# Selective-scan Mamba on one core: a later norm product, softplus's 1 + u in PSUM, the gate behind the scans, and another order of TensorE's work

## The chip, the cores and the metric

The kernel runs on 1 core of a Trainium2 chip. The metric is device time in microseconds (us), the median of the runs of one kernel. All arithmetic is fp32. The engines are TensorE (PE; its weight loads are PEld), VectorE (DVE), ScalarE (ACT), GpSimd (POOL) and SyncE (SP), whose queue issues nearly all DMAs.

## The reference

Four layers run one after the other on x of shape (4, 96, 64, 64): a fusion of two Mamba blocks (L0), a four-direction SSD Mamba (L1), the first kind again (L2), and a ConvNeXt block (L3). The change touches L0 and L2 alone. Each of these applies two Mamba blocks (`sub` 0 and 1) to 4 sequences of L = 4096 tokens and C = 96 channels, with DIN = 192 inner channels, 16 states and dt rank 6:

```python
mu = seq.mean(-1, keepdims=True)
var = ((seq - mu) ** 2).mean(-1, keepdims=True)
h = (seq - mu) * jax.lax.rsqrt(var + EPS) * ln_g + ln_b
xs, z = jnp.split(h @ in_w, 2, axis=-1)
xc = jax.nn.silu(causal_conv4(xs) + conv_b)            # depthwise, 4 taps
dbl = xc @ xproj_w                                     # dt (6), Bm (16), Cm (16)
delta = jax.nn.softplus(dbl[..., :6] @ dt_w + dt_b)
dA  = jnp.exp(delta[..., None] * A)                    # (L, 192, 16)
dBx = delta[..., None] * Bm[:, :, None, :] * xc[..., None]
hstates = scan over tokens of  h = dA * h + dBx
y = jnp.einsum('blds,bls->bld', hstates, Cm) + Dp * xc
seq = seq + (y * jax.nn.silu(z)) @ out_w
```

After the two blocks come a 1 x 1 fusion with a pooled branch, a batch norm and the residual.

## The kernel before

**Steps and groups.** `mamba_fusion` runs 32 steps (2 pairs of sequences x 2 blocks x 8 chunks of T = 512 tokens), so the two fusions have 64. A step treats two sequences at once: 2 x 192 channels are laid out as three tiles `j` of 128 rows. With 16 states, a step has 3 x 128 x 16 rows to scan. They are cut into 24 *groups* of 2 x 128 rows (`units`: tile j, then q = 0 to 3, then p = 0, 1), and the loop in `Scan.run` gives each group one *slot*. Groups with q even and p = 1 (`dma`, six of 24: numbers 1, 5, 9, 13, 17, 21) get their delta x input by a broadcasting DMA, the others by a TensorE matmul.

**What a group needs.** `load` (SP) fetches delta, broadcast over the states, into `da` (8 buffers), five slots ahead. `decay` (ACT, two slots ahead) makes exp(delta A). `spread` (one slot ahead) makes `bs` in PSUM (two tiles): four PE records at L343 or, for a dma group, two exps on ACT. `product` (POOL, L351) is for the dma groups. `scan` (DVE) multiplies `bs` by B (L369) except in dma groups, and runs two hardware scans (L374) into `hs` (4 buffers). One slot later `after` multiplies by C on POOL (L381, `hc`, 4 buffers). `sums` (PE, L400, three slots behind the scan) adds the states up into `py`, one PSUM bank, which serves one tile j at a time; for the last q it adds the D term (L394). When a tile is through, `close` (DVE, L408) reads `py` and gates it with silu(z), in place in `xz`. After j = 1 and j = 2, `project` (PE, L416 and L418) multiplies by `out_w` into the `po` bank, and `keep` (ACT, L425 or L569) brings that back to the sequence X in SBUF. `spread_out` and `reload` serve the second block only.

**The front.** In the same slots a generator, `mamba_front`, prepares the next step. The loop advances it `PACE[slot]` times a slot, where slot 0 lies LEAD slots ahead of the step's end. It centres by a matmul (`pc`), squares (ACT, L194), takes the variance by a matmul (`pv`, L184, in the `po` bank), and the root as exp(-0.5 ln) on ACT (`rs`, L111). DVE multiplies `pc` by `rs` (L178), and POOL applies gain and bias (L179). Then come 12 tap matmuls with the convolution folded into `in_w` (`pu`, L205, copied to `xz` by ACT at L210), three for z (`pz`, L215), x_proj (`pd`, L228; `dbl`), and three dt matmuls (`pt`, L269) with a softplus each. These matmuls use two `mm` banks in turn. [...]

**Softplus.** `softplus` (ACT) makes u = exp(-|x|), t = ln(1 + u), and w = 1 + u (L291). One slot later `softplus_rest` (DVE) makes max(x, 0) + t (L297) and what rounding lost in w (L299: `lg<-wa,ua`); POOL adds the two (L251), multiplies by the input (L252), and SP stores both to DRAM (`dd`, `dg`, L246), from where `load` reads them.

**What sets the order.** It is written out by hand: at the end of a slot every traced instruction is tied behind the one before it on its engine,

```python
if ins.engine in last:
    self.tc.add_manual_dep(ins, last[ins.engine].name, IN_ORDER, reason="order")
```

so each engine runs in the order in which `run` calls the stages. An engine that waits holds everything behind it.

Of the kernel before, what the change touches and what calls it, by code (L numbers as in the profile page):

```python
# [18 lines left out]
F32 = mybir.dt.float32  # L19
AF = mybir.ActivationFunctionType  # L20
ALU = mybir.AluOpType
# [4 lines left out]
B, C, HH, WW = 4, 96, 64, 64  # L26
L = HH * WW
P = 128
T = 512
# [97 lines left out]
def rsqrt(act, out, in_, eps):  # L127

    act.exp_ln(out, in_, AF.Ln, bias=eps)
    act.exp_ln(out, out, AF.Exp, scale=-0.5)  # L130
# [28 lines left out]
def mamba_front(tc, k, X, pools, wt, pair, c, h, made):  # L159

    nc = tc.nc
    work, psum, dram = pools
    if c == 0:
        nc.vector.memset(h[:C, :, 0:3], 0.0)
    else:
        nc.scalar.copy(h[:C, :, 0:3], h[:C, :, T : T + 3])

    def bank(name):
        return psum.tile([P, T], F32, tag="mm", name=name)

    centered, roots = [], []
    for n in range(4):
        if n >= 2:
            dst = h[:C, n - 2, 3 : 3 + T]
            nc.vector.tensor_tensor(dst, centered[n - 2][0], roots[n - 2], ALU.mult)  # L178
            nc.gpsimd.tensor_scalar(  # L179
                dst, dst, wt["ln"][:, 0:1], wt["ln"][:, 1:2], ALU.mult, ALU.add  # L180
            )
        if 1 <= n < 3:
            pv = psum.tile([P, T], F32, tag="po", name="pv", bufs=1)[:C]
            nc.tensor.matmul(pv, lhsT=k.mean, rhs=centered[n - 1][1], start=True, stop=True)  # L184
            rs = work.tile([P, T], F32, tag="lg", name="rs", bufs=2)[:C]
            rsqrt(k.act, rs, pv, k.eps[:C])
            roots.append(rs)
        if n < 2:
            pc = bank("pc")[:C]
            nc.tensor.matmul(  # L190
                pc, lhsT=k.center, rhs=X[:, n, ds(c * T, T)], start=True, stop=True
            )
            sq = work.tile([P, T], F32, tag="ua", name="sq", bufs=2)[:C]
            nc.scalar.activation(sq, pc, AF.Square)  # L194
            centered.append((pc, sq))
        yield


    xz = made["xz"] = work.tile([P, 6, T], F32, name="xz", bufs=2)
    for j in range(3):  # L200
        pu = bank("pu")
        for tap in range(4):
            kk = C + 1 if tap == 3 else C
            for r0, r1, d0, d1, b in SEGS[j]:
                nc.tensor.matmul(  # L205
                    pu[r0:r1], lhsT=wt["conv"][:kk, tap, d0:d1], rhs=h[:kk, b, ds(tap, T)],
                    start=(tap == 0), stop=(tap == 3),
                )
            yield
        nc.scalar.copy(xz[:, j], pu)  # L210
    k.act.other(xz[:, :3], xz[:, :3], AF.Silu)
    for j in range(3):
        pz = bank("pz")
        for r0, r1, d0, d1, b in SEGS[j]:
            nc.tensor.matmul(  # L215
                pz[r0:r1], lhsT=wt["in"][:, DIN + d0 : DIN + d1], rhs=h[:C, b, 3 : 3 + T],
                start=True, stop=True,
            )
        yield
        nc.scalar.copy(xz[:, 3 + j], pz)  # L220


    dbl = work.tile([P, T], F32, name="dbl")
    pd = bank("pd")
    for n in range(2):
        for b in range(2):
            j, r0, r1 = ROWS[b][n if b == 0 else 1 - n]
            nc.tensor.matmul(  # L228
                pd[2 * QUART * b : 2 * QUART * (b + 1)], lhsT=wt["xproj"][r0:r1, j],
                rhs=xz[r0:r1, j], start=(n == 0), stop=(n == 1),  # L230
            )
    yield
    nc.scalar.activation(dbl, pd, AF.Identity, bias=wt["one"])
    yield


    rows = dram.tile([P, T], F32, name="rows")
    bc = made["bc"] = work.tile([P, 2, 2, T], F32, name="bc", bufs=2)


    du = made["du"] = work.tile([P, 3, T], F32, name="du", bufs=2)
    kept = []
    stores = [(rows, dbl)]
    for n in range(6):
        for stored in stores:
            nc.sync.dma_start(*stored)  # L246
        stores = []
        if 2 <= n < 5:
            j = n - 2
            delta, lost = kept.pop(0)[:2]  # L250
            nc.gpsimd.tensor_tensor(delta, delta, lost, ALU.add)  # L251
            nc.gpsimd.tensor_tensor(du[:, j], delta, xz[:, j], ALU.mult)  # L252
            for name, x in (("dd", delta), ("dg", du[:, j])):
                made[name, j] = dram.tile([P, T], F32, name=f"{name}{j}")
                stores.append((made[name, j], x))
        if 1 <= n < 4:
            softplus_rest(nc, *kept[-1])
        if n == 2:
            for b in range(2):
                for q in range(2):  # L260
                    r = HALFP * b + (QUART if q else RANK + 1)
                    nc.sync.dma_start(
                        bc[:, b, q], rows[r : r + NST, None].to_broadcast([NST, HEIGHT, T])
                    )
        if n < 3:
            pt = bank("pt")
            for r0, r1, d0, d1, b in SEGS[n]:
                half = ds(HALFP * b, HALFP)
                nc.tensor.matmul(  # L269
                    pt[r0:r1], lhsT=wt["dt"][half, d0:d1], rhs=dbl[half], start=True, stop=True,  # L270
                )
            kept.append(softplus(nc, k.act, work, pt))
        if n < 5:
            yield
    k.act.other(xz[:, 3:], xz[:, 3:], AF.Silu)

PACE = (1,) * 5 + (2, 1, 1, 1) * 2 + (2,) + (1,) * 10
LEAD = 5  # L280


def softplus(nc, act, work, x):

    u = work.tile([P, T], F32, tag="ua", name="ua", bufs=2)
    t = work.tile([P, T], F32, tag="lg", name="lg", bufs=2)
    nc.scalar.activation(u, x, AF.Abs)
    act.exp_ln(u, u, AF.Exp, scale=-1.0)
    act.exp_ln(t, u, AF.Ln, bias=1.0)
    w = work.tile([P, T], F32, name="wa", bufs=2)  # L290
    nc.scalar.activation(w, u, AF.Identity, bias=1.0)  # L291
    return work.tile([P, T], F32, name="delta", bufs=2), t, u, w, x

# [8 lines left out]
class Scan:  # L302
# [126 lines left out]
    def run(self, steps, wts, front, first):  # L429

        units = [(j, q, p) for j in range(3) for q in range(NQU) for p in range(2)]
        made = [first] + [{} for _ in steps[1:]]
        groups = [
            dict(
                pair=pair, sub=sub, c=c, wt=wts[sub], made=made[n], j=j, q=q, half=p, quarters=(p, p + 2),
                first=(q == 0 and p == 0), last=(q == NQU - 1 and p == 1),
                dma=(q % 2 == 0 and p == 1),
            )
            for n, (pair, sub, c) in enumerate(steps) for j, q, p in units
        ]  # L440
        total, each = len(groups), len(units)
        ahead = iter(())
        traced = self.tc.nc.cur_bb.bb.instructions
        last = {}
        for n in range(-5, total + 9):
            start = len(traced)
            slot = (n + LEAD) % each
            if slot == 0:
                for _ in ahead:
                    pass  # L450
                step = (n + LEAD) // each + 1
                ahead = front(step, made[step]) if 0 <= step < len(steps) else iter(())

            def at(lag):
                return groups[n - lag] if 0 <= n - lag < total else None

            if (g := at(4)) and g["last"]:
                self.close(g)
            for stage, lag in (
                (self.load, -5), (self.spread, -1), (self.decay, -2), (self.after, 1),  # L460
                (self.product, -2), (self.scan, 0), (self.sums, 3),
            ):
                if g := at(lag):
                    stage(g)

            for lag, what in (
                (4, self.project), (5, self.keep), (6, self.spread_out), (7, self.reload)
            ):
                if (g := at(lag)) and g["last"] and g["j"] and (g["sub"] or lag < 6):
                    what(g, g["j"] - 1)  # L470
            for _ in range(PACE[slot] if slot < len(PACE) else 0):
                next(ahead, None)

            for ins in traced[start:]:
                if ins.engine not in self.engines:
                    continue
                if ins.engine in last:
                    self.tc.add_manual_dep(ins, last[ins.engine].name, IN_ORDER, reason="order")
                last[ins.engine] = ins
# [1093 lines left out]
```

## Time and profile before

| | |
|---|---|
| Median of 3 runs | 10014.09 us (9990.49 to 10022.18) |
| Profiled execution | 9990.73 us, span 9989.0 us |
| Busy share: DVE, PE, POOL, ACT | 82%, 85%, 70%, 55% |
| DVE scans, L374, three largest forms | 2470.1 + 819.1 + 335.7 us |
| DVE products, L369 | 1397.3 us, 1152 of 1213 ns |
| POOL hc, L381 | 3664.1 us, 1536 of 2392 ns |
| PE spread, L343, and sums, L400 | 1518.7 us and 1737.8 us |
| DVE L299, L297 | 221.0 us (192 of 1151 ns), 129.9 us (192 of 677 ns) |
| DMA | 1531.94 MB, mean 153 GB/s |

A group's row gives its count, its total busy time and the mean of one, then the idle time of its engine just before it and what ended that. The shares are over the whole span; L0 and L2 must be read from windows. [...]

### The profile page before, as it was taken

Reading aid. Unit: us, or ns where it says so; the run is one execution under the profiler, and the core shown is the slowest. Engines: PE = TensorE matmul, PEld = TensorE weight load, DVE = VectorE, ACT = ScalarE, POOL = GpSimd, SP = SyncE. Lnnn points to the kernel's source line nnn. Section 1 sums busy time; section 2 is a strip of 40 time slices with the busy share of each in tenths; the row PEclk is TensorE's granted clock in tenths of the full one; section 3 lists DMA queues with packets and bytes.
Section 4 is the critical chain, followed back from the end, with each engine's and each line's share of the span. In section 5 each row is a group of like instructions: output and inputs, shape, how many; then the busy total and the mean of one; then the engine's idle time right before and its main releaser. Section 6 shows DMA issues by size and latency. Waiting matters only on the chain. (4 is left out here: it accounts for less than half of the span.)

```text
span 9989.0 us, 110219 instructions
## 1 busy us (share of the span) xinstructions
PE 8503.0 (85%) x32896; PEld 3493.9 (35%) x32896; DVE 8183.2 (82%) x10870; ACT 5509.4 (55%) x10786; POOL 6954.8 (70%) x4573
## 2 busy tenths in 40 slices
PE   7888888888886989898889898788888888888678
PEld 1112112111122776676766767111211112112122
DVE  7999999999996666766766667699899999899887
ACT  5565665655664455555555544456566565565345
POOL 6888888888885555555555556588888888888611
PEclk8989999999997998999999999799989999899889
DMA  7777777777775222322322221777777777777653
GB/s 188 190 197 195 205 206 198 198 193 195 205 195 151 69 70 79 86 66 82 88 66 77 82 71 49 181 195 200 194 203 204 200 199 190 197 200 198 171 118 84
DMA packets 813858, 1531.94 MB, mean 153 GB/s; under 512 B 126894, under 2 KB 132426, under 8 KB 809803
## 3 DMA queue, kind: packets, MB, share of 16 engines
q1 hardware_dynamic: 810186, 1519.79, 57.7%
q8 instruction: 260, 4.26, 0.2%
q10 hardware_dynamic: 3072, 5.11, 0.1%
q14 instruction: 340, 2.78, 0.1%
HBM read 1229.28 MB, written 148.50 MB: 138 GB/s over the span
## 5 line engine op out<-in xcount | busy, mean ns | idle before, releaser
L381 POOL TENSOR_TENSOR hc<-hs,bc 128x1024 f32<-128x1024 f32 x1536 | 3664.1, 2392 | 663.9 <-DVE hs L374 654.4
L374 DVE TENSOR_TENSOR_SCAN hs<-da,carry,bs 128x512 f32<-128x512 f32 x2016 | 2470.1, 1267 | 119.5 <-DVE bs L369 3.2
L343 PE MATMUL bs<-du,seldu 64*128 64x512 f32 x4608 | 1518.7, 713 | 719.4 <-DVE hs L374 719.2
L400 PE MATMUL py<-hc,selsum 128*32 128x512 f32 x6144 | 1737.8, 650 | 9.2 <-POOL hc L381 9.2
L111 ACT ACTIVATE da<-da,w_a 128x512 f32<-128x512 f32 x2304 | 1520.1, 710 | 0.7
L369 DVE TENSOR_TENSOR bs<-bs,bc 128x1024 f32<-128x1024 f32 x1152 | 1397.3, 1213 | 66.9 <-PE bs L343 66.9
L343 PEld LDWEIGHTS bs<-du,seldu 64*128 64x128 f32 x4608 | 406.6, 202 | 1702.7 <-DVE hs L374 1128.0
L351 POOL TENSOR_TENSOR du<-du,bc 128x1024 f32<-128x1024 f32 x384 | 933.0, 2430 | 0.0
L111 ACT ACTIVATE bs<-da,w_a 128x512 f32<-128x512 f32 x768 | 529.3, 689 | 712.1 <-DVE hs L374 699.6
L1020 DVE TENSOR_SCALAR seg<-dr,dac 128x128 f32<-128x128 f32 x1536 | 637.3, 448 | 285.3 <-PE y L1065 282.7
L1036 POOL TENSOR_TENSOR seg<-seg,cb 128x384 f32<-128x384 f32 x512 | 516.3, 1010 | 478.8 <-DVE cb L1035 408.6
L205 PE MATMUL pu<-h,w_conv 96*128 96x512 f32 (+3 forms) x2048 | 825.1, 628 | 1.4 <-POOL h L179 1.4
L374 DVE TENSOR_TENSOR_SCAN hs<-bs,carry,du 128x512 f32<-128x512 f32 x672 | 819.1, 1260 | 4.3
L971 PE MATMUL front<-pk,sconv 128*128 128x512 f32 x1536 | 754.0, 608 | 25.1 <-ACT z L959 20.6
L1075 POOL TENSOR_TENSOR y<-y,xs 128x192 f32<-128x192 f32 x496 | 295.9, 596 | 604.0 <-DVE y L1074 589.6
L1088 ACT ACTIVATE y<-yz 128x192 f32<-128x192 f32 x512 | 186.1, 364 | 904.1 <-DVE yz L1087 903.3
L400 PEld LDWEIGHTS py<-hc,selsum 128*32 128x32 f32 x6144 | 227.8, 111 | 1305.9 <-issue 677.3
L1040 POOL TENSOR_TENSOR xs<-pre,coef 128x576 f32<-128x576 f32 x512 | 598.6, 1174 | 53.5 <-ACT pre L116 24.8
L982 PE MATMUL front<-sconv,pk 128*128 128x192 f32 x3072 | 572.7, 330 | 56.1 <-DVE pre L987 50.6
L982 PEld LDWEIGHTS front<-sconv,pk 128*128 128x128 f32 x3072 | 497.1, 190 | 88.3 <-DVE pre L987 77.2
L1065 PEld LDWEIGHTS y<-xs,seg 128*128 128x128 f32 x3072 | 442.0, 206 | 142.2 <-issue 83.1
L1065 PE MATMUL y<-xs,seg 128*128 128x64 f32 x3072 | 446.7, 282 | 29.4 <-POOL seg L1036 23.9
(227 smaller groups left out, 13645.7 us busy)
## 6 DMA issues: line engine op xcount, KB each, us to landing
da<-dd SPq DMA_DIRECT2D x3072, 256.0 KB
du<-dg SPq DMA_DIRECT2D x768, 256.0 KB
dr<-rows SPq DMA_DIRECT2D x256, 384.0 KB
bc<-rows SPq DMA_DIRECT2D x256, 256.0 KB
dd<-delta SPq DMA_DIRECT2D x192, 256.0 KB
dg<-du SPq DMA_DIRECT2D x192, 256.0 KB
pk<-xn SPq DMA_DIRECT2D x128, 384.0 KB
pk<-xn SPq DMA_DIRECT2D x128, 256.0 KB
```

The lines of the kernel that those rows point to most:

```text
L111: self.last = self.scalar.activation(out, in_, func, **kw)
L205: nc.tensor.matmul(pu[r0:r1], lhsT=wt["conv"][:kk, tap, d0:d1], rhs=h[:kk, b, ds(tap, T)], start=(tap == 0), stop=(tap == 3),)
L343: nc.tensor.matmul(g["bs"][:, i], lhsT=self.sel["du"][rows, g["half"], g["q"]], rhs=g["made"]["du"][rows, g["j"]], start=True, stop=True,)
L351: self.tc.nc.gpsimd.tensor_tensor(g["du"], g["du"], self.b_or_c(g, 0), ALU.mult)
L369: nc.vector.tensor_tensor(dbx, dbx, self.b_or_c(g, 0), ALU.mult)
L374: nc.vector.tensor_tensor_scan(hs[:, i], da[:, i], dbx[:, i], init, ALU.mult, ALU.add)
L381: nc.gpsimd.tensor_tensor(g["hc"], hs, self.b_or_c(g, 1), ALU.mult)
L400: nc.tensor.matmul(py[rows], lhsT=self.sel["sum"][:, g["q"]], rhs=g["hc"][:, i], start=(g["q"] == 0), stop=(g["q"] == NQU - 1),)
L971: nc.tensor.matmul(p, lhsT=self.conv[:, i, DI + q * DST : DI + (q + 1) * DST], rhs=pk[:, i, ds(c * T, T)], start=(i == 0), stop=(i == 2),)
L982: nc.tensor.matmul(p, lhsT=pk[:, i, ds(c * Q, Q)], rhs=self.conv[:, i, :DI], start=(i == 0), stop=(i == 2),)
L1020: nc.vector.tensor_scalar(seg[:, h], g["pair"]["dr"][:, c % 2 * NH + h], made["dac"][:, n0 + h : n0 + h + 1], 0.0, ALU.subtract, ALU.min,)
L1065: nc.tensor.matmul(py[:, ch], lhsT=seg[:, h], rhs=xs[:, 0, ch], start=True, stop=True)
```

## The change

- In `mamba_front` the variance and roots come two turns behind the centring, and the product two turns behind the roots (six turns in place of four).
- `softplus` writes 1 + u into the PSUM bank `po` in place of an SBUF tile (`wa`).
- In the loop `close` moves behind `scan`. `keep`, `spread_out`, `reload` come one slot later and ahead of the front's work; `sums` moves behind the front's work, and `project` behind `sums` and one slot later.
- LEAD is 4 in place of 5, PACE follows, and the loop has one more slot at its end.

```diff
@@ -172,16 +172,16 @@
         return psum.tile([P, T], F32, tag="mm", name=name)
 
     centered, roots = [], []
-    for n in range(4):
-        if n >= 2:
-            dst = h[:C, n - 2, 3 : 3 + T]
-            nc.vector.tensor_tensor(dst, centered[n - 2][0], roots[n - 2], ALU.mult)
+    for n in range(6):
+        if n >= 4:
+            dst = h[:C, n - 4, 3 : 3 + T]
+            nc.vector.tensor_tensor(dst, centered[n - 4][0], roots[n - 4], ALU.mult)
             nc.gpsimd.tensor_scalar(
                 dst, dst, wt["ln"][:, 0:1], wt["ln"][:, 1:2], ALU.mult, ALU.add
             )
-        if 1 <= n < 3:
+        if 2 <= n < 4:
             pv = psum.tile([P, T], F32, tag="po", name="pv", bufs=1)[:C]
-            nc.tensor.matmul(pv, lhsT=k.mean, rhs=centered[n - 1][1], start=True, stop=True)
+            nc.tensor.matmul(pv, lhsT=k.mean, rhs=centered[n - 2][1], start=True, stop=True)
             rs = work.tile([P, T], F32, tag="lg", name="rs", bufs=2)[:C]
             rsqrt(k.act, rs, pv, k.eps[:C])
             roots.append(rs)
@@ -269,25 +269,25 @@
                 nc.tensor.matmul(
                     pt[r0:r1], lhsT=wt["dt"][half, d0:d1], rhs=dbl[half], start=True, stop=True,
                 )
-            kept.append(softplus(nc, k.act, work, pt))
+            kept.append(softplus(nc, k.act, work, psum, pt))
         if n < 5:
             yield
     k.act.other(xz[:, 3:], xz[:, 3:], AF.Silu)
 
 
 
-PACE = (1,) * 5 + (2, 1, 1, 1) * 2 + (2,) + (1,) * 10
-LEAD = 5
-
-
-def softplus(nc, act, work, x):
+PACE = (1,) * 6 + (2, 1) * 5 + (1,) * 8
+LEAD = 4
+
+
+def softplus(nc, act, work, psum, x):
 
     u = work.tile([P, T], F32, tag="ua", name="ua", bufs=2)
     t = work.tile([P, T], F32, tag="lg", name="lg", bufs=2)
     nc.scalar.activation(u, x, AF.Abs)
     act.exp_ln(u, u, AF.Exp, scale=-1.0)
     act.exp_ln(t, u, AF.Ln, bias=1.0)
-    w = work.tile([P, T], F32, name="wa", bufs=2)
+    w = psum.tile([P, T], F32, tag="po", name="w", bufs=1)
     nc.scalar.activation(w, u, AF.Identity, bias=1.0)
     return work.tile([P, T], F32, name="delta", bufs=2), t, u, w, x
 
@@ -442,7 +442,7 @@
         ahead = iter(())
         traced = self.tc.nc.cur_bb.bb.instructions
         last = {}
-        for n in range(-5, total + 9):
+        for n in range(-5, total + 10):
             start = len(traced)
             slot = (n + LEAD) % each
             if slot == 0:
@@ -454,22 +454,27 @@
             def at(lag):
                 return groups[n - lag] if 0 <= n - lag < total else None
 
-            if (g := at(4)) and g["last"]:
-                self.close(g)
             for stage, lag in (
                 (self.load, -5), (self.spread, -1), (self.decay, -2), (self.after, 1),
-                (self.product, -2), (self.scan, 0), (self.sums, 3),
+                (self.product, -2), (self.scan, 0),
             ):
                 if g := at(lag):
                     stage(g)
-
-            for lag, what in (
-                (4, self.project), (5, self.keep), (6, self.spread_out), (7, self.reload)
-            ):
-                if (g := at(lag)) and g["last"] and g["j"] and (g["sub"] or lag < 6):
-                    what(g, g["j"] - 1)
+            if (g := at(4)) and g["last"]:
+                self.close(g)
+
+            def completed(*stages):
+
+                for lag, what, subs in stages:
+                    if (g := at(lag)) and g["last"] and g["j"] and g["sub"] in subs:
+                        what(g, g["j"] - 1)
+
+            completed((6, self.keep, (0, 1)), (7, self.spread_out, (1,)), (8, self.reload, (1,)))
             for _ in range(PACE[slot] if slot < len(PACE) else 0):
                 next(ahead, None)
+            if g := at(3):
+                self.sums(g)
+            completed((5, self.project, (0, 1)))
 
             for ins in traced[start:]:
                 if ins.engine not in self.engines:
```

## The prediction

> **What bounds the kernel now.** I read the stage table first. The selective-scan part (the two `mamba_fusion` calls, about 100 to 3150 and 6400 to 9400 us) is two thirds of the span, and only it is touched. In it DVE is the busiest engine, and every engine is below its limit:
>
> ```profile
> 100.00:3000.00 2900.00, 2494.76 (x7600) 572.17 (x7598) 2647.72 (x2340) 1734.27 (x3249) 2437.49 (x1152) 0.91 0.75 198
> ```
>
> (Columns: length, busy us of PE, PEld, DVE, ACT, POOL, then clock, DMA share, GB/s.) DVE is busy for 91%, PE for 86%, POOL for 84%. Next, what DVE waits for, in the first fusion:
>
> ```profile
> DVE h L178 <- ACT rs L111: 70.1, 52, 3.1
> DVE xz L408 <- PE py L400: 53.1, 92, 4.5
> DVE bs L369 <- PE bs L343: 35.0, 53, 1.6
> DVE delta L297 <- ACT lg L111: 24.7, 30, 1.1
> ```
>
> The second fusion answers with 66.3, 60.1, 31.9 and 24.3. Together DVE stands 136 us at the norm's product, 113 at the gate, 67 at the scan's product and 49 at softplus: 365 us, 5.7 us for each of the 64 steps. A step takes 95.1 us (gate to gate, 3013.1 us for 760 groups of the first fusion, 24 groups a step). Third, the DVE timeline of one step, for what one group costs (start, duration, idle before):
>
> ```profile
> 1028.47 2.45 DVE L374 TENSOR_TENSOR_SCAN hs<-da,carry,bs 128x512 f32<-128x512 f32 x2
> 1030.84 2.43 DVE L374 TENSOR_TENSOR_SCAN hs<-bs,carry,du 128x512 f32<-128x512 f32 x2
> 1035.32 0.69 DVE L178 TENSOR_TENSOR h<-pc,rs 96x512 f32<-96x512 f32 x1 [2.04 <-ACT rs L111]
> 1036.84 1.23 DVE L369 TENSOR_TENSOR bs<-bs,bc 128x1024 f32<-128x1024 f32 x1 [0.83 <-PE bs L343]
> 1038.11 2.45 DVE L374 TENSOR_TENSOR_SCAN hs<-da,carry,bs 128x512 f32<-128x512 f32 x2
> ```
>
> From start to start a pair of scans takes 2.36 and a product 1.31, so a group costs 3.68, and 2.36 if it is one of the six of 24 fed by DMA. The 2.04 and 0.83 are one event. Fourth, PE's timeline tells why:
>
> ```profile
> 1014.64 2.08 PE L343 MATMUL bs<-du,seldu 64*128 64x512 f32 x4 [6.49 <-DVE hs L374]
> 1020.51 1.27 PE L343 MATMUL bs<-du,seldu 64*128 64x512 f32 x4
> 1032.74 1.10 PE L184 MATMUL pv<-sq,mean 96*96 96x512 f32 x2 [3.02 <-ACT X L569]
> ```
>
> The variance matmul `pv` shares the single `po` bank with `project`; it waits until ACT's `keep` has emptied it, ACT takes two roots' steps, and DVE, which owes the product one slot later, stands behind both. Behind its 6.49 us of idleness PE runs at half rate (2.08 for four records, then 1.27).
>
> [...] L299 (`w` and `u` in SBUF) takes 681 to 2890 ns, mean 1151; L297, the same form with one operand in PSUM, 662 to 693. Beside L299 POOL's `hc` takes 2.80 instead of 2.36. [...]
>
> **The change, part by part.** A group's slot is named by its number n in the step (0 to 23); the DMA groups are 1, 5, 9, 13, 17, 21.
>
> *Norm's product two slots behind its roots.* `pv` moves one slot further from `keep`, the roots stay with it, and L178 falls into slots 0 and 1, at least a whole slot after the second ACT step. ACT needs about 1.3 us for two steps, in a slot of 3.7. No instruction is added. Gain: all of the 136 us. POOL's L179 goes with it; POOL already waits there for DVE.
>
> *Gate at the slot's end.* L408 runs behind the scan of the same slot (2.4 to 3.7 us later), while its last sums were issued a slot before. In slots 3 and 19 PE is through; in 11 it is a tie. The cost is a wait of the next tile's first `sums` (one `py` bank) for this gate; `sums` and the next spread, about 2 us, fit into the following DVE slot. Gain 95 of 113; bounds 53 and 113.
>
> *1 + u in PSUM.* 192 instructions L299 of 1151 ns become like L297's 677: 192 x 0.474 = 91 us of DVE. [...] ACT's write to PSUM costs nothing: `bs<-da` takes 689 where `da<-da` takes 710. New wait: `w` of j+1 needs the bank that L299 of j reads, so ACT stands until that slot's end. Behind it on ACT are the exps of DMA group 17 (1.4 us), due a slot of 5 us later: covered. POOL's stretched `hc` come back to 2.36, off the path.
>
> *LEAD 4, new PACE.* The `dt` matmuls now follow slot 13, which has no front matmul, so ACT's logarithm is early: 40 of the 49 us at L297 go (bounds 0 and 49). Front, stores and loads of `bc` fall one slot later against the loads of `da`. On SP's queue the four `bc` loads (1 MB) now stand behind the two transfers of group 21 and right ahead of `dd`'s first store; that store frees the buffer that the third L297 writes, some 3 us later, where in the timeline shown there were 4.0 (1010.53 to 1014.54). That wait exists now (4.2 us, 4 times). I take 0.3 us a step, 19 us; bounds 0 and 1 us, 64.
>
> *Front's matmuls ahead of the sums, `project` a slot later.* The same work in another order; what comes late next is the spread. At full rate a spread is 1.06, a group's sums 0.98, a front matmul about 1.05, `project` 3.1: 77 us a step. From slot 2 to 12 PE holds 41 us against DVE's 39 (with one slot of lead), and slot 20, behind the gate of 19, 5.1 us. Added up slot by slot this leaves DVE 0.5 at group 6, 0.4 at 11, 1.1 at 22: 2.0 us a step[...]. Now it is 67/64 = 1.05. I take 2.2: 74 us more; bounds 0 and 205. ACT's copy of `pu` (L210) waits for `project` to free `xz`, 10.4 us a step now (312.1 in the first fusion) without hurting; that stays hidden.
>
> DVE work after it: 18 x 3.68 + 6 x 2.36 + 5 short ones (L178, L408) at 0.61 + 3 x (0.77 + 0.61) for softplus = 88 us; POOL 79, PE 77, so DVE stays the bound. DMA's 18.3 MB a step need 203 GB/s instead of 192; single windows of 4 us show 260 to 330, so loads stay covered. The extra slot at each fusion's end has only leftovers.
>
> **Sum:** 136 + 95 + 91 + 40 - 19 - 74 = 269 us. The profiled execution took 9990.7 (span 9989.0): 9722. The median of runs, 10014.1, lies 23 above it and the three spread over 32; I allow 8 and say 9730.
>
> **Rivals.** *A, PE becomes the bound.* For it: 77 of 90 us of work, dense stretches, half rate after waits; against it: PE waits 360 us for DVE in the first fusion alone. At the upper ends (205 and 64), with the gate at 53 and L297 at 0, it is 136 + 53 + 91 - 269 = 11 us: 9980 in this execution, 9988 in the median. Half of the way there, about 9860, is the likelier form.
>
> *B, ACT is caught behind `project`: slower.* L210 in slot 4 now stands in front of the exps of group 7, and `project` stands behind two front matmuls and the sums. PE's slots 2 to 4 hold 13.4 us from scan 1's end; exps of group 7 would be done at 15.3 and are due at 19.0. At half rate through all three slots PE ends at 26.8, exps at 28.7: 9.7 us lost a step, 621 in all, hence 9722 + 621 = 10343, 10350 as a median. It decides from a `project` 3.7 us late; from 8 us late the gain is gone. [...]
>
> *C, the waits only move.* If the DVE waits reflect an equal PE chain, they reappear at L369 and only L299's 91 us remain: 9900 in this execution, 9907 as a median.
>
> **How the numbers follow.** Forecast 0.58, A 0.20 (a fifth of it, 0.04, within 0.3% of no change), C 0.10, B 0.12 with any form that ends slower. A measurement of this kernel tells 0.3%, 30 us, from nothing. Faster 0.58 + 0.16 + 0.10 = 0.84, same 0.04, slower 0.12. The low end takes every saving whole, 136 + 113 + 91 + 49 = 389, and no new wait: 9602, say 9600. The high end, 9935, takes in C and most of A, and leaves out B and A's tail.
>
> **What would show it.** Right: L178's and L408's idle near nothing, L299 near 0.68 with a narrow spread, step of about 91 us, DVE above 94% in this stage. Wrong: idle at L369 above 250 us (A or C), L297 waiting for the store of `dd`, or exps on ACT with DVE's scan behind them and L210 waiting far over 10 us a step (B).

## The result and the profile after

The changed kernel is slower by 0.4%: 10046.9 us as a median (10025.03 to 10061.92, 14 runs) against 10009.18 of the kernel before (14 runs), a ratio of 1.0041, 95% interval 1.0031 to 1.0051. The forecast was 9730. The profiled execution's span is 10041.4 us, 52 above that of before; in the first fusion (100 to 3130 us) DVE is busy for 88%, where it was 91%.

What DVE waited for, first fusion, in the changed kernel (line waiting, what released it, us in total, times, longest), all but the smallest:

```profile
DVE bs L369 <- PE bs L343: 193.6, 70, 5.6
DVE delta L297 <- DMA dd<-delta: 81.5, 29, 4.1
DVE delta L297 <- POOL du L252: 4.3, 2, 2.2
```

The row of L299 among the groups (busy us, mean ns; 221.0 and 1151 before):

```profile
L299 DVE SCALAR_TENSOR_TENSOR lg<-w,ua 128x512 f32<-128x512 f32 x192 | 132.9, 692 | 20.4 <-ACT ua L111 0.5 <-DVE delta L297 0.5
```

The three waits that the change was aimed at are gone (L178's 136 us, 109 of the gate's 113, the 49 for ACT at L297), and L299 fell from 221.0 to 132.9 us. Two other waits took their place. In both fusions L369 waits 378 us for PE, where it was 67, and the third L297 of a step waits 167 us for the store of `dd`, where it was 4. DVE's busy time fell by 122 us (8183.2 to 8060.8), and its idle time at L178, L297, L369 and L408 together rose from 369 to 555; 186 - 122 = 64 us, against 52 of the span.

**The wait at L369.** Counted group by group, nearly all of it stands in front of two groups of each step: 181 us before group 6 and 193 before group 22. PE now waits for the gate, which it did not before. PE's waits at L400 in the first fusion, before the change and after it:

```profile
PE py L400 <- POOL hc L381: 4.6, 3, 2.6
```

```profile
PE py L400 <- DVE xz L408: 112.8, 59, 3.2
```

PE around slot 3's gate in the changed kernel (start, duration, idle before):

```profile
1068.48 1.12 PE L205 MATMUL pu<-h,w_conv 96*128 96x512 f32 x2
1070.37 1.05 PE L400 MATMUL py<-hc,selsum 128*32 128x512 f32 x4 [0.77 <-DVE xz L408]
1071.35 2.14 PE L205 MATMUL pu<-h,w_conv 97*128 97x512 f32 x6
1073.42 1.05 PE L400 MATMUL py<-hc,selsum 128*32 128x512 f32 x4
1074.40 1.10 PE L416 MATMUL po<-X,fus 96*96 96x512 f32 x2
1075.43 2.12 PE L418 MATMUL po<-xz,w_out 64*96 64x512 f32 x4
1077.48 1.13 PE L343 MATMUL bs<-du,seldu 64*128 64x512 f32 x4
```

And DVE in the same microseconds:

```profile
1069.56 0.67 DVE L408 TENSOR_TENSOR xz<-py,xz 128x512 f32<-128x512 f32 x1
1070.14 1.22 DVE L369 TENSOR_TENSOR bs<-bs,bc 128x1024 f32<-128x1024 f32 x1
1071.49 2.45 DVE L374 TENSOR_TENSOR_SCAN hs<-da,carry,bs 128x512 f32<-128x512 f32 x2
1073.86 2.43 DVE L374 TENSOR_TENSOR_SCAN hs<-bs,carry,du 128x512 f32<-128x512 f32 x2
1078.66 1.23 DVE L369 TENSOR_TENSOR bs<-bs,bc 128x1024 f32<-128x1024 f32 x1 [2.37 <-PE bs L343]
```

The gate is the last thing in slot 3. The first sums of the next tile need its bank `py`, so PE starts them at 1070.37; behind them stand slot 4's taps, its sums, `project`, and only then the spread of group 6. That is 8 us of PE behind the gate, while DVE has 6 us to do, since group 5 is one of the short DMA groups. The same happens behind the gate of slot 19, before group 22. There PE stands longer, and starts at half rate (four sums in 1.92 us where they took 1.05 above; granted clock 0.50 from 1035.6 to 1042.3 us):

```profile
1038.99 1.92 PE L400 MATMUL py<-hc,selsum 128*32 128x512 f32 x4 [3.15 <-DVE xz L408]
1040.84 1.85 PE L190 MATMUL pc<-X,center 96*96 96x512 f32 x2
```

**The wait at L297.** In the kernel before, SP issues the first store of `dd`, and DVE starts the third L297, which writes the same buffer, 4.0 us later and without a wait:

```profile
1010.53 0.53 SPq L246 DMA_DIRECT2D dd<-delta  x1
```

```profile
1014.54 0.69 DVE L297 SCALAR_TENSOR_TENSOR delta<-pt,lg 128x512 f32<-128x512 f32 x1
```

In the changed kernel, SP's issues, then the third L297:

```profile
1018.52 3.19 SPq L262 DMA_DIRECT2D bc<-rows  x4
1022.38 1.16 SPq L326 DMA_DIRECT2D da<-dd  x2
1023.63 0.53 SPq L246 DMA_DIRECT2D dd<-delta  x1
```

```profile
1029.47 0.69 DVE L297 SCALAR_TENSOR_TENSOR delta<-pt,lg 128x512 f32<-128x512 f32 x1 [3.41 <-DMA dd<-delta]
```

Meanwhile the DMA engines are busy without a break (each row has the stretch and its length, the busy us of PE, PEld, DVE, ACT and POOL, then clock, DMA share, GB/s):

```profile
1016.60:1019.60 3.00, 1.83 (x8) 0.44 (x6) 2.90 (x4) 2.00 (x4) 3.00 (x2) 1.00 0.43 128
1019.60:1022.60 3.00, 0.61 (x4) 0.23 (x4) 2.90 (x4) 2.94 (x7) 2.92 (x3) 0.88 1.05 257
1022.60:1026.00 3.40, 3.40 (x6) 0.77 (x6) 3.30 (x4) 3.31 (x7) 3.40 (x3) 0.50 1.08 259
```

From issue to release the 256 KB store took 5.8 us, behind 1 MB of `bc` and 0.5 MB of `da`. Around the store of the kernel before the share was lower:

```profile
1008.00:1012.00 4.00, 0.15 (x2) 0.00 (x0) 3.90 (x5) 3.53 (x6) 3.92 (x3) 0.82 0.60 148
```

### The profile page after: what moved, and what is told of

Read it like the earlier page. It is cut to its first block, busy times and chain, and to the rows that moved or that the text cites. A ratio compares the mean times of both kernels' runs of the same rounds, so it can differ in the third digit from the quotient of the medians.

```text
span 10041.4 us, 110079 instructions
## 1 busy us (share of the span) xinstructions
PE 8451.2 (84%) x32896; PEld 3485.0 (35%) x32896; DVE 8060.8 (80%) x10870; ACT 5551.0 (55%) x10786; POOL 6873.5 (68%) x4573
## 4 chain that ended last, share of the span: by engine, by line
PE 50%; DVE 28%; ACT 7%; issue 6%; DMA 4%; POOL 3%; SPq 1%; DVEq 0%; POOLq 0%; ACTq 0%
DVE hs L374 12%; PE py L400 9%; PE bs L343 7%; PE pu L205 6%; PE front L976 6%; DVE bs L369 5%; PE front L987 3%; DMA dd<-delta 3%; PE po L418 3%; PE y L1070 2%; DVE seg L1025 2%; PE pz L215 2%; DVE yz L1092 2%; PE pc L190 2%; DVE acc L1370 2%
## 5 line engine op out<-in xcount | busy, mean ns | idle before, releaser
L381 POOL TENSOR_TENSOR hc<-hs,bc 128x1024 f32<-128x1024 f32 x1536 | 3617.1, 2357 | 1045.2 <-DVE hs L374 993.8
L343 PE MATMUL bs<-du,seldu 64*128 64x512 f32 x4608 | 1463.5, 690 | 700.0 <-DVE hs L374 699.2
L400 PE MATMUL py<-hc,selsum 128*32 128x512 f32 x6144 | 1687.7, 657 | 234.6 <-DVE xz L408 221.3
L369 DVE TENSOR_TENSOR bs<-bs,bc 128x1024 f32<-128x1024 f32 x1152 | 1399.5, 1215 | 407.7 <-PE bs L343 407.0
L351 POOL TENSOR_TENSOR du<-du,bc 128x1024 f32<-128x1024 f32 x384 | 905.6, 2358 | 49.2 <-DMA du<-dg 49.2
L400 PEld LDWEIGHTS py<-hc,selsum 128*32 128x32 f32 x6144 | 224.0, 112 | 1527.2 <-issue 1146.7
L384 ACT COPY carry<-hs 128x2 f32<-128x2 f32 x1344 | 247.4, 184 | 737.2 <-DVE hs L374 735.4
```

The source lines that it names most:

```text
L343: nc.tensor.matmul(g["bs"][:, i], lhsT=self.sel["du"][rows, g["half"], g["q"]], rhs=g["made"]["du"][rows, g["j"]], start=True, stop=True,)
L351: self.tc.nc.gpsimd.tensor_tensor(g["du"], g["du"], self.b_or_c(g, 0), ALU.mult)
L369: nc.vector.tensor_tensor(dbx, dbx, self.b_or_c(g, 0), ALU.mult)
L381: nc.gpsimd.tensor_tensor(g["hc"], hs, self.b_or_c(g, 1), ALU.mult)
L400: nc.tensor.matmul(py[rows], lhsT=self.sel["sum"][:, g["q"]], rhs=g["hc"][:, i], start=(g["q"] == 0), stop=(g["q"] == NQU - 1),)
```

## The experiments

All ratios are to the kernel before, run on the same chip beside them. Theory 1: two separate late chains, the store of `dd` and the one behind the gate. Theory 2: PE is full, so a wait removed comes back at L369. Theory 3: the new place of the front's matmuls is to blame.

**Three buffers for delta.**

```diff
-    return work.tile([P, T], F32, name="delta", bufs=2), t, u, w, x
+    return work.tile([P, T], F32, name="delta", bufs=3), t, u, w, x
```

> The changed kernel with three buffers for delta in place of two. Theory 1 (two separate late chains): the third L297 no longer waits for the store of dd; its 167 us over both fusions go, L369 keeps about 380 us of waiting for PE; 9880 us, ratio to before about 0.988. Theory 2 (PE is full and sets the pace): DVE arrives earlier and waits as much longer at L369; 10030 to 10060 us, ratio 1.00.

Measured: 9874.9 us, ratio 0.9871 (0.9856 to 0.9887). The wait for the store is gone and L369 stays at 373 us (378). From 1.0041 this is 170 us, as much as the wait; none of it moved to L369. For this wait theory 1 holds, and theory 2 does not.

**The gate at the slot's start again.**

```diff
+            if (g := at(4)) and g["last"]:
+                self.close(g)
             for stage, lag in (
...
-            if (g := at(4)) and g["last"]:
-                self.close(g)
```

> The changed kernel with the gate (L408) back at the start of its slot, the rest as changed. Theory 1 (the first sums of a tile wait for the gate in py's only bank, and project and the next spread stand behind them): L369 falls from 378 to 100 us or less, the gate's own wait rises from 4 to 100 to 200 us, L297's 167 us stay; 9880 to 9960 us, ratio 0.987 to 0.995. Theory 2 (PE is full): L369 keeps over 300 us and the gate's wait comes on top; ratio above 1.01.

Measured: 9996.44 us, ratio 0.9988 (0.9978 to 0.9997). First fusion, waits of DVE:

```profile
DVE xz L408 <- PE py L400: 151.5, 65, 4.4
DVE delta L297 <- DMA dd<-delta: 85.6, 30, 3.8
DVE bs L369 <- PE bs L343: 9.1, 20, 2.4
```

L369 falls from 378 to 18 us over both fusions, so the gate's place makes that wait. But the gate now waits 296 us itself, more than the 113 of the kernel before: most of the wait has moved, and that both can go is shown only by the runs below. The last sums of a tile, for which the gate waits, now come behind the front's matmuls. The gain of some 50 us is less than expected: the direction was right, the size of the gate's wait was not.

**The gate between product and scans.** L369 gets a function of its own, and `close` comes between the two.

```diff
-                (self.product, -2), (self.scan, 0),
+                (self.product, -2), (self.times_b, 0),
...
             if (g := at(4)) and g["last"]:
                 self.close(g)
+            if g := at(0):
+                self.scan(g)
```

> The changed kernel with the gate between its slot's product (L369) and its scans, 2.4 us earlier than at the slot's end. Theory 1: the gate's wait stays under 40 us and L369 falls from 378 to about 100 us; 9770 to 9830 us, ratio 0.977 to 0.983. Theory 2 (PE is full): L369 keeps over 300 us, ratio 1.00.

Measured: 9880.8 us, ratio 0.9876 (0.986 to 0.9893). L369 waits 97 us, as expected; the gate still waits 158, where under 40 were expected, and the time is 51 us above the expected range. About 101 us of the gate's wait fall in slot 11, behind slot 10's `pz` matmuls and the sums that follow them, and 52 in slot 3.

**Sums and `project` ahead of the front.**

```diff
+            if g := at(3):
+                self.sums(g)
+            completed((5, self.project, (0, 1)))
             for _ in range(PACE[slot] if slot < len(PACE) else 0):
                 next(ahead, None)
-            if g := at(3):
-                self.sums(g)
-            completed((5, self.project, (0, 1)))
```

> The changed kernel with sums and project back ahead of the front's matmuls. Theory 1 (project and the spread stand behind the gate through py): it helps nothing, since two front matmuls more now stand between the gate and the spread of group 6: L369 grows by 60 to 130 us, ratio 1.01 to 1.02. Theory 3 (front's matmuls ahead of the sums are what makes the sums, project and so the spread late): L369 falls below 150 us, ratio 0.98 to 0.99.

Measured: 10166.24 us, ratio 1.0164 (1.0148 to 1.0179). L369 rises to 498 us. Theory 3 falls: with the gate at the slot's end, having the front's matmuls ahead of `sums` and `project` is a help worth 120 us.

**1 + u in PSUM alone, in the kernel before.**

```diff
-    w = work.tile([P, T], F32, name="wa", bufs=2)
+    w = psum.tile([P, T], F32, tag="po", name="w", bufs=1)
```

> The kernel before with 1 + u in the po bank, nothing else of the change. Theory 1 (each edit's saving is real; it was lost elsewhere): L299 near 0.68 us in the place of 1.15, 91 us less; 9910 us, ratio 0.991. If instead DVE's time isn't what sets the pace (theory 2): ratio 1.00, with the 91 us back as waits at L369 or L408.

Measured: 9972.97 us, ratio 0.9969 (0.9957 to 0.9981). L299's group falls from 221.0 to 132.8 us, but the time by 31 us. In the profiled execution L178 waits 178 us (136), L369 118 (67), L297 for the store 15 (4), the gate 64 (113). Here neither theory gave the right size: DVE arrives earlier, the roots and the spread don't follow, and about two thirds of what L299 saves come back as waits. That the other edits of the change would free them was not run apart.

**Both mends: three delta buffers, and the gate between product and scans.** The edits are the two shown above, put together.

> The changed kernel with both: three buffers for delta, and the gate between product and scans. Theory 1 says that the two losses are separate and add: 0.9871 + 0.9876 - 1.0041 = 0.971, 9710 us. Theory 2 (PE is full): less than half of the second gain appears, ratio 0.979 or more.

Measured: 9727.08 us, ratio 0.9718 (0.9701 to 0.9734). The two gains taken alone add up to 0.9706, close to that: the two losses are separate.

**A tile's last sums ahead of the front.** Added to the former:

```diff
+            if (g := at(3)) and g["last"]:
+                self.sums(g)
             for _ in range(PACE[slot] if slot < len(PACE) else 0):
                 next(ahead, None)
-            if g := at(3):
+            if (g := at(3)) and not g["last"]:
                 self.sums(g)
```

> The former (three delta buffers, gate between product and scans) with the sums of a tile's last group alone ahead of the front's matmuls, since the gate waits for just those. Theory 1: the gate's wait of 158 us falls below 50, L369 stays near 95; 9610 to 9640 us, ratio 0.961 to 0.964. Theory 2: what goes at the gate comes back at L369, ratio as without it.

Measured: 9626.24 us, ratio 0.9619 (0.9605 to 0.9634). The gate's wait is down to 8 us from 180 in the kernel it was added to; L369's went from 81 to 168, not staying near 95 as theory 1 had it. What is left at L369 lies mainly at group 6 (134 us), then at group 22 (31), behind `project`.

**`bc` behind the stores of group 17's slot.**

```diff
-        if n == 2:
+        if n == 3:
             for b in range(2):
                 for q in range(2):
```

> The changed kernel with the four bc loads one front turn later, behind the stores of dd0 and dg0 on SP's queue; delta keeps two buffers. If the store of dd is late because 1 MB of bc loads stands ahead of it in full DMA queues: the wait at L297 falls from 167 to 60 us or less, ratio 0.993 to 0.996. If it is late only because the third softplus now follows a DMA group, whose slot is 1.3 us shorter: the wait stays above 120 us, ratio 1.000 to 1.004.

Measured: 10049.86 us, ratio 1.0035 (1.0021 to 1.005). The wait at L297 falls from 167 to 94 us, between the two expectations: the 1 MB ahead of the store is part of it. The rest may be the closer succession of the L297; no run shows it. The time hardly moves, and L369 rises from 378 to 440 us. Why here, and not with three delta buffers, is not settled.

**Idle matmuls that keep PE busy.** Five matmuls a step from constants into the free `po` bank, whose result nobody reads: two in slot 18, one in 19, two in 0; once on the best kernel so far, once on the changed one.

```diff
+WARM = {18: 2, 19: 1, 0: 2}
...
+                pw = self.psum.tile([P, T], F32, tag="po", name="warm", bufs=1)
+                for _ in range(WARM[n % each]):
+                    self.tc.nc.tensor.matmul(
+                        pw, lhsT=self.k.ident,
+                        rhs=self.sel["du"][:, 0].rearrange("p q m -> p (q m)"), start=True, stop=True,
+                    )
...
```

> The best kernel so far (three delta buffers, gate between product and scans, a tile's last sums ahead of the front) with five matmuls (128x512) a step whose result nobody reads, in PE's empty places: two in slot 18, one in 19, two in 0. If PE's half rate after idle places is what makes group 22's spread late: L369's 168 us fall below 80, 9540 to 9580 us, ratio 0.953 to 0.957. If it is only the chain of gate, sums, project and spread: L369 stays at 150 us or more, ratio 0.962 or above.

Measured: 9518.75 us, ratio 0.9512 (0.949 to 0.9533), the fastest version. L369 waits 80 us, and the mean granted clock of the profiled execution rose from 0.925 to 0.946. Of the 88 us that went, 57 lay before group 6 and 29 before group 22. So more than half of what was left at L369, 88 of 168 us, went as the granted clock rose.

> The changed kernel with the same five idle matmuls a step. If half rate carries a large part of its 378 us at L369: below 280, ratio 0.992 to 0.996. If the chain behind the gate at the slot's end carries it: above 340, ratio 1.000 to 1.006.

Measured: 10104.32 us, ratio 1.0101 (1.0076 to 1.0126), and L369 at 465 us: slower still than either expectation had it. The profiled execution is the slowest of the four (10145.3 us, the others 10096 to 10106). Before group 22, whose spread stands behind the slots with three of the five matmuls, the wait fell from 193 to 93 us; before group 6 it rose from 181 to 355. PE's timeline at slot 3's gate (the line numbers are one higher here):

```profile
1065.48 1.13 PE L205 MATMUL pu<-h,w_conv 96*128 96x512 f32 x2
1068.80 1.26 PE L401 MATMUL py<-hc,selsum 128*32 128x512 f32 x4 [2.20 <-DVE xz L409]
1069.99 3.98 PE L205 MATMUL pu<-h,w_conv 97*128 97x512 f32 x6
1073.91 1.92 PE L401 MATMUL py<-hc,selsum 128*32 128x512 f32 x4
```

PE stands 2.20 us in front of the gate instead of 0.77, and then runs the taps in 3.98 us instead of 2.14 (granted clock 0.50 from 1072 to 1076 us). Group 6 waits 5.56 us instead of 2.37. In the changed kernel, over both fusions, only 8 of 52 such waits in front of slot 3's gate had six taps of over 3 us behind them. Behind slot 19's gate the first four sums took 1.9 us there in all 60 cases; in this step, behind a wait of 2.17 us, they take 1.05, and half rate comes later (1.92 for the next four). So the gate at the slot's end does two things: it delays the work behind it, and the idle place in front of it can put that work at half rate. In the kernel with all three mends, the gate 2.4 us earlier among them, PE never waits for the gate, and the same five matmuls gain 107 us (0.9619 to 0.9512). That the gate alone makes this difference was not run apart.

## Why the prediction was wrong

- **The bound** was read rightly: DVE sets the pace in this stage, and DVE's waits are what can be gained. Rival C (the waits merely move, with PE's chain equal) has the right sign of the trouble at L369, but three delta buffers gave their whole 170 us, and the later runs went down to 9519 us, so these waits could be taken away without coming back. In part it holds for the kernel before: of L299's 88 us alone, 31 became time.
- **The savings** all came in the profile: 136 expected at L178 and 136 measured; 95 and 109 at the gate; 91 and 88 at L299; 40 and 49 at L297. Their sum of 382 us was even above the 362 forecast. That each of them would also become time was taken for granted by the forecast, and for L299 alone it was not so.
- **The first step that failed** is "`sums` and the next spread, about 2 us, fit into the following DVE slot". Two things are wrong in it. Behind the gate stand front's matmuls and `project` too, 8 us and not 2. And the table by slots counted PE's work from slot 2 to 12 as if it ran through "with one slot of lead"; the wait for `py` in slot 3 takes that lead away. I had called slots 3 and 19 harmless because PE is through with the tile's last sums by then; that is why the gate doesn't wait, and just why PE waits for the gate. The term was 2.2 us a step; the upper bound of 205 us more makes 4.25 a step with the 1.05 of before. It measured 5.9 (378/64).
- **Half rate** was allowed for in that upper bound once a step, as an estimate of the author. The runs with idle matmuls show that it is not an addition of fixed size. With them L369's wait at group 22 halved (193 to 93 us), and at group 6, where the half rate then fell on the work in front of `project`, it doubled (181 to 355). The prediction saw half rate behind 6.49 us of idleness; it followed shorter idleness too, 3.02 us in the same trace (four records of a spread in 2.08 us at 1034.71, clock 0.50 from 1034.5 to 1037.9 us) and 2.20 us here.
- **The second step that failed** is the store of `dd`: the edge was named (queue, 1 MB of `bc` ahead, 3 us), and sized at 0.3 us a step, at most 1. It measured 2.6. The 4.0 us in the trace of before were a time in which the store had finished, not its duration, and the store was issued where the DMA share was low (0.60 at 148 GB/s from 1008 to 1012 us); at the new place it is 1.05 to 1.08. And the third L297 fell behind DMA group 17, whose slot is shorter by a product of 1.31 us; what that adds was not run apart.
- **Rival B**: ACT's L210 waited for `project` 172 us in the first fusion, where it was 312, and DVE waited there for no exp of ACT: it was not this.
- **Rival A's upper ends** gave 9980 and the measured loss went beyond them: 311 us more at L369 against 205, and 163 more at L297 against 64. Taken at its measured sizes, the sum of the four savings and the two waits is 382 - 311 - 163 = -92, slower, where the span says -52. Of the rest, about 40 us, 34 are that DVE's busy time fell by 122 us and not by L299's 88 alone; where these 34 lie was not followed up.

Mended in the two places, the edits give what was forecast for them: 9727 us with three delta buffers and the gate between product and scans, where 9730 stood in the forecast. That is the sum of other terms than the forecast had, and no confirmation of it.

## What to carry to other kernels

When an instruction is moved to a later place to spare its own engine a wait, follow the buffer that it frees: write down who waits for that buffer, and everything queued behind that waiter until the next thing that the first engine needs. A table of work by slots has to carry these waits from slot to slot, else it grants a lead that isn't there. And a distance in a trace in which a transfer was not late is only an upper bound of its time there; ask how busy the DMA engines are at the new place (here 1.05 to 1.08, where it was 0.60).

## What was unexpected of the hardware

Standing idle for 2.20 us was enough here for PE to run at half rate soon after (taps in 3.98 us instead of 2.14), and 0.77 us was not. The record of the granted clock, which is 1.0 or 0.5 throughout in the traces of both kernels, before and after, bears this out. In the changed kernel PE stood 76 times in front of a gate while at full clock: half rate began during none of the 44 waits of 0.4 to 0.8 us or in the 47 us after them, and for all 32 of 2.2 us or more it began during the wait or within 1.5 us of its end. The length of one wait doesn't settle it, though. In the kernel before, over both fusions, half rate began during PE's waits at full clock or within 2 us of their end for none of 52 of 0.3 to 1.6 us, 23 of 32 of 1.7 to 1.9 us, 57 of 61 of 2.1 to 2.3 us, 43 of 61 of 2.7 to 3.0 us, and all 71 of 5.3 us or more. And in the kernel with a tile's last sums ahead of the front, four sums took 1.92 us behind a wait of 0.68 us, where PE had stood idle for 2.05 us just before. So five matmuls of no use made one kernel faster by 107 us and another slower by 57 (1.0041 to 1.0101), and in the slower one they still halved the wait at group 22.

The effect of PSUM on L299 was forecast, and as the only edit it came just so: of two SBUF operands, the move of one to PSUM took 40% off the instruction (1151 to 692 ns), so that the mean now lies near the former minimum of 681.
